# A cross-attention block: all of W1 by seven products, and PSUM as one tile

## The chip, the cores and the metric

The kernel runs on one core of a Trainium2 chip. The metric is the device time of one execution in microseconds (us). The engines named are TensorE (PE; its weight loads are shown apart as PEld), VectorE (DVE), ScalarE (ACT), GpSimd (POOL) and SyncE (SP, which only issues DMAs). All arithmetic is fp32.

## The reference

128 sequences of 128 tokens, 256 features, 16 heads of 16; a strictly causal mask (a token sees only earlier ones, and the first row of the attention is zero); two layer norms and a feed-forward part of width 1024.

```python
q = (query @ Wq + bq).reshape(b, s, 16, 16).transpose(0, 2, 1, 3)   # k, v from ctx alike
scores = jnp.einsum('bhqd,bhkd->bhqk', q, k) / sqrt(16)
scores = jnp.where(j < i, scores, -1e30)
attn = softmax(scores); attn[:, :, 0, :] = 0
ctx = jnp.einsum('bhqk,bhkd->bhqd', attn, v)
x = layer_norm(query + ctx @ Wo + bo, ln1_g, ln1_b)
ffn = jax.nn.relu(x @ W1 + b1) @ W2 + b2
out = layer_norm(x + ffn, ln2_g, ln2_b)
```

## The kernel before

The work goes by pairs of sequences, p = 0 to 63, 256 tokens each. Every engine's instructions run in the order of the program text (a manual schedule), with semaphores between engines; no engine runs anything ahead of what stands before it in its own queue. The stages of a pair are spread over several steps. `step(p)` is the steady part, for p = 7 to 62, and once more with `last` true for p = 63; in it stand

- `weigh(p-2)` and `context(p-2)`: attention weights times values into PSUM bank 7, copied by ScalarE;
- `scores_both(p)`: scores of pair p. The "high" half (queries 64 to 127 of each sequence) goes to banks 0 to 3, the "low" half (queries 0 to 63) to banks 6, 7, 4 and 5, four heads to a bank. TensorE writes banks 4 and 5 first, then 0 and 1, then 2 and 3, and 6 and 7 last;
- the masks and maxima on VectorE (`mask` for the low half, `mask_high` for the high half, `low_maximum`), and the exponentials by head on ScalarE, which also add up the sums of the softmax;
- projections: queries (bank 4) and keys (bank 0) of pair p+1, the attention's output of pair p-2 (bank 5), values of pair p (bank 1);
- `sums`: VectorE takes reciprocals, GpSimd multiplies the exponentials by them (the division of the softmax), in two parts of eight heads for the high half and in one for the low half;
- `turn`: VectorE transposes the weights in 32x32 blocks, twice for the high half (parts 0 and 1) and once for the low half; `bring` is 16 DMAs on SP's queue that finish this transposition, and it stands behind the `store` of an older pair;
- `norm1(p-2)` on ScalarE, and `turn_x1(p-2)`, a transposition of x1 on VectorE followed by five DMAs through DRAM;
- the feed-forward part. W2 of pair p-4 goes by seven products instead of eight (the Winograd form of Strassen's 2x2 scheme): GpSimd makes four sums `hS` of blocks of the hidden layer (`combine_hidden`), TensorE makes seven products of four 128x128x128 matmuls each into banks 6 and 7 (`second_by_seven`, with no-operations between the matmuls), VectorE adds them up (`sum_of_seven`). W1 of pair p-3 goes by seven products for half of its eight blocks of 128 hidden features: `NI = 2`, four sums `xS` of x1 on GpSimd (`combine_normed`), combinations `w1t` of the weights made once, products of two 128x128x128 matmuls, two products to a bank (banks 2 to 5; `Hidden.run`), and additions into `hT` on VectorE (`u2`, `u3`, `rest`). The other half of the blocks is plain, 256 columns at a time, into banks 0, 1, 2 and 0 (`Hidden.plain`). ScalarE applies bias and relu, to the plain blocks out of PSUM, to the others in place.

The relus of two of the blocks by seven products stand in the next step, behind `context`. PSUM's eight banks are eight tiles (`at_bank`). The steps ahead of 7 and the code behind 63 (`behind`) do the same work with other queues' orders.

Of the kernel before, what the change touches and what calls it, by code (L numbers as in the profile page):

```python
# [8 lines left out]
F32 = mybir.dt.float32  # L9
# [10 lines left out]
def tile_cross_attention_block(  # L20
# [188 lines left out]

    def at_bank(i, name):  # L210
        return psum.tile([P, 512], F32, tag=f"b{i}", name=name)
# [155 lines left out]
    def scores_both(p):  # L367

        st = states[p]
        for hi in range(2):  # L370
# [22 lines left out]
    def mask(p, hi, rs):  # L393
        st = states[p]
        n = P if hi else HP
        no = neg.rearrange("p u j -> p (u j)") if hi else neg[:, 1, :]
        for r in rs:
# [41 lines left out]


# [182 lines left out]
    b1s = const.tile([P, DFF // NS], F32, tag="b1s", name="b1s")  # L623
# [75 lines left out]
    def hidden(p, fs, between=None, banks=(2, 3, 4, 0)):  # L699
# [3 lines left out]
        for f in fs[::2]:  # L703
# [4 lines left out]
            for i in range(2):  # L708
                for k in range(KC):
# [5 lines left out]
                    if p == 1:  # L715
                        empty(3 if f else 2)
# [32 lines left out]
    def mask_high(p, rs):  # L749

        st = states[p]
        for r in rs:
            ps = st["sps", 1][r].rearrange("p (n j) -> p n j", j=P)
            nc.vector.tensor_tensor(
                ps[:, :, HP:], ps[:, :, HP:], neg[:, 1, None, :].to_broadcast([P, 4, HP]), ALU.add
            )
        for r in rs:
            nc.vector.tensor_reduce(  # L758
                st["nmx", 1][:, 4 * r : 4 * r + 4],
                st["sps", 1][r].rearrange("p (n j) -> p n j", j=P), AX.X, ALU.max, negate=True,  # L760
            )
# [5 lines left out]
    def exponential_by_head(p, hi, heads, summed=False):  # L767

        st = states[p]
        if summed and ("su", hi) not in st:  # L770
            st["su", hi] = small.tile([P, H], F32, tag=f"sa{hi}", name=f"sa{hi}_{p}")
# [28 lines left out]
    def second_by_seven(p):  # L800
# [3 lines left out]
        py = st["py"] = at_bank(6, f"py_{p}")  # L804
        pz = st["pz"] = at_bank(7, f"pz_{p}")
# [14 lines left out]
        product(py[:, :P], raw(0, 0), weights(0, 0), 7)  # L820
        product(pz[:, :P], raw(1, 0), weights(1, 0), 7)
        product(pz[:, 2 * P : 3 * P], raw(1, 1), lambda k: wt[:, 3, k], 7)
        product(py[:, 3 * P :], lambda k: hs[:, 0, k], lambda k: wt[:, 0, k], 7)
        product(py[:, 2 * P : 3 * P], lambda k: hs[:, 2, k], lambda k: wt[:, 2, k], 7)
        product(py[:, P : 2 * P], lambda k: hs[:, 1, k], lambda k: wt[:, 1, k], 7)
        product(pz[:, P : 2 * P], lambda k: hs[:, 3, k], weights(1, 1), 6)

    def sum_of_seven(p):

        st = states[p]  # L830
        t2 = st["t2"] = ffn.tile([P, 2, D], F32, tag="t2", name=f"t2_{p}", bufs=3)
        t = t2.rearrange("p s (h d) -> p (s h) d", h=2)
        py, pz = st.pop("py"), st.pop("pz")
        x1b = st.pop("x1b").rearrange("p s (h d) -> p (s h) d", h=2)
# [7 lines left out]
        add(t, x1b, 0)  # L842
# [7 lines left out]
    NI = 2  # L850
# [20 lines left out]
    class Hidden:  # L871

        WHERE = {1: (2, 0), 6: (2, 1), 7: (3, 0), 4: (3, 1), 2: (4, 0), 3: (4, 1), 5: (5, 0)}
# [8 lines left out]
        def of(self, which, n=1):  # L882
            at, n0 = self.WHERE[which]
            if at not in self.banks:
                self.banks[at] = at_bank(at, f"phs_{self.p}_{at}")
            return self.banks[at][:, n0 * NI * P : (n0 + n) * NI * P]

# [29 lines left out]
        def rest(self):  # L917
# [3 lines left out]
            )  # L921
            low = self.h[:, :, 0]
            nc.vector.tensor_tensor(
                low, low, self.of(2, 2).rearrange("p (e i t) -> p e i t", e=2, i=NI), ALU.add
# [49 lines left out]
    bvw = const.tile([P, KC, P], F32, tag="bvw", name="bvw")  # L974
# [257 lines left out]
    def fall_in(p):  # L1232

        weigh(p - 2)
        context(p - 2)
        scores_both(p)
        second_sum(1)
# [6 lines left out]
        mask_high(p, A)  # L1244
        exponential_by_head(p, 1, ONES)
        mask_high(p, B)
# [287 lines left out]
```

## Time and profile before

| | |
|---|---|
| time, median of 3 runs | 1520.04 us (1518.93 to 1522.97) |
| the profiled execution | 1522.34 us; its span, first to last instruction, 1520.5 us |
| mean granted clock of TensorE | 0.998 |
| busy share of the span | TensorE 99%, weight loads 89%, GpSimd 89%, ScalarE 85%, VectorE 84% |
| the largest parts of the chain that ended last | plain W1 (L938) 13%, W2 products (L809) 13% and 10%, W1 by seven products (L899) 11% |

In a row of a timeline stand the start in us, the duration, engine, line, operation, output and inputs, shapes and the count of instructions merged in it; in square brackets the idle time ahead of it and what ended that. A row of waits reads: who waited, for whom, us in total, times, the longest. One fp32 matmul stands as two records.

### The profile page before, as it was taken

What the parts mean: (1) busy time and instruction counts of PE and PEld (TensorE: products, weight loads), DVE (VectorE), ACT (ScalarE), POOL (GpSimd) and SP (SyncE); (2) the same over time, 40 slices, a digit from 0 to 9 for tenths busy, and PEclk for the clock granted to TensorE, in tenths of its full rate; (3) what the DMA queues carried; (4) which work ended last, traced back from release to release, by engine and by line L of the source; (5) the groups of instructions that cost most, each with busy time, mean ns of one, the idle gap of its engine ahead of it and who ended that gap; (6) DMA issues with size and microseconds to landing.
All of it is one profiled execution on the core that took longest, in us unless ns stands there. A gap on an engine that the chain in (4) does not pass through costs nothing.

```text
span 1520.5 us, 53525 instructions
## 1 busy us (share of the span) xinstructions
PE 1506.5 (99%) x18598; PEld 1359.2 (89%) x18598; DVE 1281.6 (84%) x2607; ACT 1295.0 (85%) x5271; POOL 1358.2 (89%) x1510
## 2 busy tenths in 40 slices
PE   8999999999999999999999999999999999999998
PEld 7788998999999989989989999899899899999987
DVE  7989888888888888888888888888888888888775
ACT  5668988988988989989889889899899898898862
POOL 6878999999999999999999999999999999999983
PEclk9999999999999999999999999999999999999999
DMA  9456665655655656656566566556565666664441
GB/s 196 91 113 144 147 151 139 138 133 135 141 142 138 131 140 135 147 138 135 134 137 142 141 140 129 142 133 150 134 140 131 139 137 146 138 132 124 108 119 47
DMA packets 415314, 204.59 MB, mean 135 GB/s; under 512 B 282448, under 2 KB 383056, under 8 KB 415056
## 3 DMA queue, kind: packets, MB, share of 16 engines
q1 hardware_dynamic: 412768, 199.34, 56.9%
q8 instruction: 158, 2.59, 0.8%
q10 hardware_dynamic: 2288, 1.85, 0.5%
q14 instruction: 100, 0.82, 0.2%
HBM read 70.26 MB, written 33.29 MB: 68 GB/s over the span
## 4 chain that ended last, share of the span: by engine, by line
PE 92%; DVE 3%; ACT 2%; POOL 1%; DMA 1%; SPq 1%; issue 1%; ACTq 0%; POOLq 0%; DVEq 0%
PE ph L938 13%; PE py L809 13%; PE phs L899 11%; PE pz L809 10%; PE pq L261 7%; PE po L523 7%; PE pv L301 7%; PE pk L261 6%; PE pss L384 6%; PE pc L504 4%; PE ph L710 3%; PE pc L494 2%; ACT sm L775 1%; SPq L462 1%; POOL sm L434 1%
## 5 line engine op out<-in xcount | busy, mean ns | idle before, releaser
L775 ACT ACTIVATE sm<-pss,nmx 128x128 f32<-128x128 f32 x944 | 328.5, 405 | 87.1 <-POOL hS L795 74.9
L434 POOL TENSOR_TENSOR sm<-sm,rs 128x1024 f32<-128x1024 f32 x192 | 362.1, 1900 | 3.4 <-DVE rs L433 3.3
L447 DVE STREAM_TRANSPOSE tb<-sm 128x1024 f32<-128x1024 f32 x186 | 223.4, 1226 | 110.9 <-POOL sm L434 90.7
L775 ACT ACTIVATE sm<-sm,nmx 128x64 f32<-128x64 f32 x944 | 313.7, 404 | 0.0
L775 ACT ACTIVATION_READ_ACCUMULATOR sm<-sm,nmx 128x1 f32 x912 | 235.1, 258 | 0.0
L775 ACT ACTIVATION_READ_ACCUMULATOR sm<-pss,nmx 128x1 f32 x912 | 223.3, 245 | 0.0
L938 PE MATMUL ph<-x1T,w 128*128 128x256 f32 x896 | 213.8, 386 | 0.1
L938 PEld LDWEIGHTS ph<-x1T,w 128*128 128x128 f32 x896 | 161.3, 190 | 36.1 <-ACT vd L324 18.8
L809 PE MATMUL py<-wt,hS 128*128 128x128 f32 x1440 | 171.2, 275 | 1.0 <-DVE hS L796 0.5
L809 PEld LDWEIGHTS py<-wt,hS 128*128 128x128 f32 x1440 | 165.8, 192 | 1.4 <-DVE hS L796 0.7
L758 DVE TENSOR_REDUCE nmx<-pss 128x4 f32<-128x512 f32 x236 | 150.9, 680 | 0.0
L398 DVE TENSOR_TENSOR sm<-pss,neg 128x256 f32<-128x256 f32 (+1 forms) x276 | 108.3, 435 | 34.9 <-PE pss L384 32.0
L928 ACT ACTIVATE hT<-ph,b1e_c 128x256 f32<-128x256 f32 x224 | 98.8, 465 | 35.5 <-PE ph L938 35.5
L291 ACT ACTIVATE kT<-pk,bkh,half 128x256 f32<-128x256 f32 x252 | 123.7, 609 | 4.0 <-PE pk L261 4.0
L261 PE MATMUL pq<-xT,wq 128*128 128x256 f32 x504 | 125.4, 392 | 0.5 <-DVE sm L398 0.5
L523 PE MATMUL po<-wo,cxT 128*128 128x256 f32 x512 | 121.3, 380 | 0.7 <-ACT cxT L516 0.7
L301 PE MATMUL pv<-wv,cT 128*128 128x256 f32 x512 | 120.9, 379 | 0.0
L261 PE MATMUL pk<-cT,wk 128*128 128x256 f32 x504 | 119.2, 379 | 0.0
L795 POOL TENSOR_TENSOR hS<-hT 128x512 f32<-128x512 f32 x57 | 72.2, 1267 | 50.2 <-ACT hT L928 50.1
L523 PEld LDWEIGHTS po<-wo,cxT 128*128 128x128 f32 x512 | 96.9, 190 | 14.4 <-ACT cxT L516 1.2
L261 PEld LDWEIGHTS pq<-xT,wq 128*128 128x128 f32 x504 | 90.7, 189 | 20.8 <-issue 9.8
L301 PEld LDWEIGHTS pv<-wv,cT 128*128 128x128 f32 x512 | 97.2, 190 | 13.2
(164 smaller groups left out, 3987.4 us busy)
## 6 DMA issues: line engine op xcount, KB each, us to landing
pT<-tb SPq DMA_DIRECT2D x976, 96.0 KB, 2.2
x1t<-tbx SPq DMA_DIRECT2D x252, 64.0 KB, 1.8
x1T<-x1t SPq DMA_DIRECT2D x63, 256.0 KB, 2.9
out_dram<-t SPq DMA_DIRECT2D x63, 256.0 KB, 2.4
xb<-in_x_dram SPq DMA_DIRECT2D x124, 128.0 KB, 3.8
cb<-in_ctx_dram SPq DMA_DIRECT2D x124, 128.0 KB, 3.8
x<-in_x_dram SPq DMA_DIRECT2D x31, 512.0 KB, 4.6
w<-in_L_xattn_W_dram SPq DMA_DIRECT2D x2, 1024.0 KB, 7.7
```

What stands on the lines that cost most here:

```text
L261: nc.tensor.matmul(ps[:, m * TP : (m + 1) * TP], w[:, k, m * P : (m + 1) * P], src[:, k, :], start=(k == 0), stop=(k == KC - 1),)
L291: nc.scalar.activation(st["kT"][:, m, e, :], pk[:, m * TP : (m + 1) * TP], AF.Identity, bias=bkh[:, m, e : e + 1], scale=half[:, e : e + 1],)
L301: nc.tensor.matmul(pv[:, s * D : (s + 1) * D], st["cT"][:, k, s * P : (s + 1) * P], wv[:, k, :], start=(k == 0), stop=(k == KC - 1),)
L398: nc.vector.tensor_tensor(st["sm", hi][:, 4 * r : 4 * r + 4, :], st["sps", hi][r][:, : 4 * n].rearrange("p (n j) -> p n j", j=n), no[:, No ...
L434: nc.gpsimd.tensor_tensor(sm[:, part, :], sm[:, part, :], rs[:, :, None].to_broadcast([P, part.stop - part.start, n]), ALU.mult,)
L447: nc.vector.transpose(st["tb"][:, :, at : at + 256].rearrange("p j (n a) -> p n j a", a=32), st["sm", hi].rearrange("p h j -> p (h j)")[:, ...
L523: nc.tensor.matmul(po[:, s * D : (s + 1) * D], cxT[:, k, s, :], wo[:, k, :], start=(k == 0), stop=(k == KC - 1),)
L758: nc.vector.tensor_reduce(st["nmx", 1][:, 4 * r : 4 * r + 4], st["sps", 1][r].rearrange("p (n j) -> p n j", j=P), AX.X, ALU.max, negate=True,)
L775: nc.scalar.activation(sm[:, h, :], src, AF.Exp, bias=nmx[:, h : h + 1], scale=1.0, **({"accum_out": st["su", hi][:, h : h + 1]} if summed ...
L809: nc.tensor.matmul(out, left(k), right(k), start=(k == 0), stop=(k == FC // 2 - 1))
L899: nc.tensor.matmul(ps[:, i * P : (i + 1) * P].rearrange("p (n a) -> p n a", a=32), left(i), right, start=True, stop=True,)
L938: nc.tensor.matmul(self.plains[f].rearrange("p (s i a) -> p s i a", s=2, a=32), w1[:, k, f * P : (f + 1) * P], self.x1T[:, :, :, k, :], st ...
```

## The change

- `NI = 4`: all eight blocks of W1 go by seven products, each product four 128x128x128 matmuls that fill one bank. The plain blocks are gone from the steps. `rest` is split in `add2`, `add3` and `add5`. The additions are twice as wide. Relus of the even blocks stand in the same step, those of the four odd blocks in the next one behind `context`.
- All of PSUM is one tile, `banks`, of which `at_bank` gives slices. With it the low mask of banks 6 and 7 is one instruction, and so are the mask and the maximum of the high half in banks 2 and 3; in banks 0 and 1 each maximum now follows its own mask.
- The first W2 product has bank 2 for itself and is added early (`first_of_seven`), ahead of the other sums.
- `sums` becomes `inverse` (one reciprocal for 16 heads) and `divide`. The order in the step changes: the high divisions stand ahead of the deviation and the shift of the first norm, `norm1` and `turn_x1` stand within the hidden stage, the low division behind `residual1`, `add_bo` behind the low division, the second high transposition ahead of the sums, the low one ahead of `add5`.
- Fewer no-operations in the W2 products (48 to 22 a step); two early tiles share the place of `hS`.

```diff
+    banks = psum.tile([P, 8, 512], F32, tag="banks", name="banks")
     def at_bank(i, name):
-        return psum.tile([P, 512], F32, tag=f"b{i}", name=name)
+        return banks[:, i]
...
+        if not hi and rs[0] == 0 and "both" in st:
+            r = rs[0]
+            at = (6, 4)[r // 2]
+            nc.vector.tensor_tensor(
+                st["sm", 0][:, 4 * r : 4 * r + 8, :].rearrange("p (b n) j -> p b n j", b=2),
+                banks[:, at : at + 2, : 4 * n].rearrange("p b (n j) -> p b n j", j=n),
+                no[:, None, None, :].to_broadcast([P, 2, 4, n]), ALU.add,
+            )
+            return
...
+    def inverse(p, hi):
+        st = states[p]
+        rs = st["rs", hi] = small.tile([P, H], F32, tag=f"rs{hi}", name=f"rs{hi}_{p}")
+        nc.vector.reciprocal(rs, st["su", hi])
+    def divide(p, hi, part):
+        st = states[p]
+        sm = st["sm", hi]
+        nc.gpsimd.tensor_tensor(
+            sm[:, part, :], sm[:, part, :],
+            st["rs", hi][:, part, None].to_broadcast([P, part.stop - part.start, sm.shape[2]]),
+            ALU.mult,
+        )
...
-    def mask_high(p, rs):
...
+    def mask_high(p, first, n):
+        st = states[p]
+        ps = banks[:, first : first + n].rearrange("p b (n j) -> p (b n) j", j=P)
+        nc.vector.tensor_tensor(
+            ps[:, :, HP:], ps[:, :, HP:], neg[:, 1, None, :].to_broadcast([P, 4 * n, HP]), ALU.add
+        )
+        nc.vector.tensor_reduce(
+            st["nmx", 1][:, 4 * first : 4 * (first + n)], ps, AX.X, ALU.max, negate=True,
+        )
...
-        product(py[:, :P], raw(0, 0), weights(0, 0), 7)
+        product(px[:, :P], raw(0, 0), weights(0, 0), 3)
...
+    def first_of_seven(p):
+        st = states[p]
+        st["t2"] = ffn.tile([P, 2, D], F32, tag="t2", name=f"t2_{p}", bufs=3)
+        nc.vector.tensor_tensor(
+            st["t2"].rearrange("p s (h d) -> p (s h) d", h=2),
+            st.pop("x1b").rearrange("p s (h d) -> p (s h) d", h=2),
+            st.pop("px")[:, None, :P].to_broadcast([P, 4, P]), ALU.add,
+        )
...
-    NI = 2
+    NI = 4
...
-        WHERE = {1: (2, 0), 6: (2, 1), 7: (3, 0), 4: (3, 1), 2: (4, 0), 3: (4, 1), 5: (5, 0)}
+        WHERE = {1: 2, 6: 3, 7: 4, 4: 5, 2: 0, 3: 1, 5: 6}
...
+        def add2(self):
+            nc.vector.tensor_tensor(self.h[:, 0, 0], self.h[:, 0, 0], self.one(2), ALU.add)
+        def add3(self):
+            nc.vector.tensor_tensor(self.h[:, 1, 0], self.h[:, 1, 0], self.one(3), ALU.add)
+        def add5(self):
...
         h.keep()
-        stack_values(p)
+        values_out(p)
         h.u2()
         h.run(7)
         h.run(4)
         h.u3()
+        norm1(p - 2)
+        norm2(p - 5)
+        turn_x1(p - 2)
         h.run(2)
+        h.add2()
         h.run(3)
+        h.add3()
+        for f in (0, 2, 4, 6):
+            h.relu(f)
+        turn(p, 0, 0)
         h.run(5)
-        h.rest()
-        norm2(p - 5)
-        h.plain([4], 0)
-        h.relu(4)
...
+        h.add5()
...
-            for f in range(NI, 2 * NI):
+            for f in (1, 3, 5, 7):
                 states[p - 4]["rest"].relu(f)
...
-        sums(p, 1, ONE)
-        sums(p, 1, TWO)
+        inverse(p, 1)
+        divide(p, 1, ONE)
+        divide(p, 1, TWO)
+        if not last:
+            deviation(p - 2, 1)
+            shift(p - 2, 1)
...
-        second_by_seven(p - 4)
+        second_by_seven(p - 4, None if last else 2)
         if not last:
-            sums(p, 0, ALL)
+            first_of_seven(p - 4)
+            turn(p, 1, 1)
         residual1(p - 3)
         sum_of_seven(p - 4)
-        if last:
-            sums(p, 0, ALL)
+        inverse(p, 0)
+        divide(p, 0, ALL)
         if not last:
-            turn_x1(p - 2)
-            spread_values(p)
+            add_bo(p - 1)
+        if not last:
             hidden_by_seven(p)
```

More of the change, by code (lines that the diff above doesn't have):

```diff
@@ L622, in tile_cross_attention_block @@
     b1e_c = const.tile([P, FC], F32, tag="b1e_c", name="b1e_c")
-    b1s = const.tile([P, DFF // NS], F32, tag="b1s", name="b1s")
+    early = ffn.tile([P, 4, FC // 2, P], F32, tag="hS", name="early", bufs=1)
+    b1s = early[:, 1, : DFF // NS // P].rearrange("p k f -> p (k f)")
     def fold_norm1():
@@ L804, in second_by_seven @@
         py = st["py"] = at_bank(6, f"py_{p}")
+        px = st["px"] = py if apart is None else at_bank(apart, f"px_{p}")
         pz = st["pz"] = at_bank(7, f"pz_{p}")
@@ L880, in __init__, with of @@
             self.banks, self.plains = {}, {}
[L882 to L886, printed above, removed]
+        def of(self, which):
+            if which not in self.banks:
+                self.banks[which] = at_bank(self.WHERE[which], f"phs_{self.p}_{which}")
+            return self.banks[which][:, : NI * P]
         def run(self, which):
@@ L972, in tile_cross_attention_block @@
     nc.vector.tensor_scalar(bqs_c, bq_c, QSCALE, None, ALU.mult)
-    bvw = const.tile([P, KC, P], F32, tag="bvw", name="bvw")
+    bvw = early[:, 0, :KC]
     nc.vector.memset(bvw[:, :, 0:1], 0.0)
@@ L1360, in step @@
         combine_hidden(p - 4, POOL_ALONE)
-        add_bo(p - 1)
-        if not last:
+        if last:
+            add_bo(p - 1)
+        else:
             combine_normed(p - 3)
@@ L1389, in step @@
         else:
-            norm1(p - 2)
             keys(p + 1)
             values(p)
-        sums(p, 1, ONE)
-        sums(p, 1, TWO)
+        inverse(p, 1)
+        divide(p, 1, ONE)
+        divide(p, 1, TWO)
+        if not last:
+            deviation(p - 2, 1)
+            shift(p - 2, 1)
         if p + 2 < NP:
@@ L1418, in step @@
             hidden(p - 3, range(FC))
-        turn(p, 0, 0)
-        if not last:
+        if last:
+            turn(p, 0, 0)
+        else:
             finish(p - 5)
@@ L1447, in behind @@
             scale_and_shift(p - 3)
+            finish(p - 4)
+            store(p - 4)
         norm2(p - 3)
```

75 lines of the change are left out of this document (27 added, 48 removed).

## The prediction

> **What bounds the kernel now.** First the page: how long, and which engine is busy.
>
> ```profile
> span 1520.5 us, 53525 instructions
> ...
> PE 1506.5 (99%) x18598; PEld 1359.2 (89%) x18598; DVE 1281.6 (84%) x2607; ACT 1295.0 (85%) x5271; POOL 1358.2 (89%) x1510
> ```
>
> TensorE is busy throughout, but its busy time is modelled, so I looked at one step of the steady part (`step(31)`) and at the whole steady part by windows.
>
> ```profile
> core 0: us, PE busy (x) PEld busy (x) DVE busy (x) ACT busy (x) POOL busy (x), PEclk, DMA share, GB/s
> 698.60:721.76 23.16, 23.16 (x293) 21.07 (x292) 19.78 (x42) 20.84 (x88) 21.44 (x25) 1.00 0.64 149
> 142.50:1439.71 1297.21, 1297.09 (x16353) 1179.95 (x16353) 1106.19 (x2294) 1166.34 (x4927) 1198.17 (x1345) 1.00 0.60 137
> ```
>
> From 142.50 to 1439.71 the kernel makes the 56 steps of p = 7 to 62 in 1297.21 us, 23.16 each, at full clock, and the step shown takes exactly that. The waits inside that step, by who sat idle, for VectorE and GpSimd:
>
> ```profile
> DVE tb L447 <- POOL sm L434: 1.9, 1, 1.9
> DVE sm L398 <- PE pss L384: 0.5, 1, 0.5
> DVE hT L911 <- ACT hT L908: 0.3, 1, 0.3
> POOL hS L795 <- ACT hT L928: 0.9, 1, 0.9
> ```
>
> TensorE has no row there; the others wait for it or for each other: VectorE 2.7 us of 23.16, GpSimd 0.9. So TensorE's own stream sets the step, but GpSimd's queue is full to 22.26 and VectorE's to 20.46. TensorE's timeline of the step, and one weight-load row:
>
> ```profile
> 698.29 0.38 PE L938 MATMUL ph<-x1T,w 128*128 128x256 f32 x1
> 698.60 0.43 PE L494 MATMUL pc<-pT,vd 128*32 128x64 f32 x16
> ...
> 701.63 1.99 PE L261 MATMUL pq<-xT,wq 128*128 128x256 f32 x8
> 703.46 1.89 PE L523 MATMUL po<-wo,cxT 128*128 128x256 f32 x8
> 705.19 1.89 PE L261 MATMUL pk<-cT,wk 128*128 128x256 f32 x8
> ...
> 714.00 1.06 PE L809 MATMUL pz<-w,hS 128*128 128x128 f32 x8
> 714.89 0.61 PE L899 MATMUL phs<-x1T,w 128*128 128x128 f32 x4
> ...
> 718.02 3.82 PE L938 MATMUL ph<-x1T,w 128*128 128x256 f32 x16
> 721.76 0.43 PE L494 MATMUL pc<-pT,vd 128*32 128x64 f32 x16
> 718.98 2.46 PEld L938 LDWEIGHTS ph<-x1T,w 128*128 128x128 f32 x12 [0.33 <-ACT vd L324]
> ```
>
> Read the starts. One fp32 matmul is two records. 128 columns: 8 records from 714.00 to 714.89, 0.112 us each. 256 columns: 8 from 703.46 to 705.19, 0.216 each. W1 is the stretch 714.89 to 721.76.
>
> **TensorE's part of the change.** Removed are the 16 wide records of the plain blocks (718.02 to 721.76, 3.74 us); added are 28 narrow ones, as many as stand in 714.89 to 718.02, so 3.13 us. Of the 3.74, 3.46 is 16 x 0.216. Some of the rest is the wait for the values' copies (0.33 on the weight loads, `vd`, bank 1), which goes; the rest is the hand-over to the next stage, 698.29 to 698.60 = 0.31 against 0.216, so 0.09, which stays. Gain 3.74 - 3.13 - 0.09 = **0.52 us a step, floor 22.64**. The product that now takes bank 1 after the values comes 4.5 us into W1, where the second plain block came after 4.1, and norm1 no longer stands ahead of those copies. The no-operations in the W2 products, cut from 48 to 22 a step, I cost at nothing either way: 8 padded records (714.00) and the unpadded W1 records stand equally 0.112 apart.
>
> **VectorE.** Rows of the same step:
>
> ```profile
> 700.89 0.76 DVE L398 TENSOR_TENSOR sm<-pss,neg 128x256 f32<-128x256 f32 x2 [0.53 <-PE pss L384]
> 706.05 1.22 DVE L765 TENSOR_REDUCE nmx<-sm 128x16 f32<-128x1024 f32 x1
> 709.15 0.66 DVE L247 STREAM_TRANSPOSE xT<-xb 128x512 f32<-128x512 f32 x1
> 718.85 0.42 DVE L914 TENSOR_TENSOR hT<-hT,phs 128x256 f32<-128x256 f32 x1
> 719.83 0.69 DVE L919 TENSOR_TENSOR hT<-hT,phs 128x512 f32<-128x512 f32 x1
> 720.56 0.69 DVE L923 TENSOR_TENSOR hT<-hT,phs 128x512 f32<-128x512 f32 x1
> 721.16 2.36 DVE L447 STREAM_TRANSPOSE tb<-sm 128x1024 f32<-128x1024 f32 x2
> ```
>
> Three additions into `hT` go from 256 to 512 elements (0.42 to 0.69): +0.81. L919 goes from 512 to 1024; no 1024 addition from PSUM is in the trace: between 1.22 (the 1024 reduction) and 2 x 0.69 = 1.38. I take 1.22, since 256 to 512 added only 0.27: +0.53. L923 becomes two of its size: +0.69. Together +2.03. Saved: one mask, one mask and one maximum of the high half, one reciprocal, at most 0.1 each, since two masks back to back take 0.76 against 0.69 for one double one; given back, because each high maximum now follows its own mask at once. I count zero. VectorE needs 20.46 + 2.03 = 22.5 of 22.64: it fits by 0.15, so its order decides.
>
> The **VectorE loop**: the query projection writes bank 4, so it waits for the low mask, which stands behind all that VectorE has from the step before. From 701.63 to the first W1 record at 714.89 is 13.26; four products of 8 records 3.58; the last record outlives its successor's start by 0.17 (1.06 against 0.89); hand-over 0.08. At 17.09 VectorE may do the second half of u3, and behind it in its queue: transposition of x1 0.60 (0.66 of L247, less what two rows overlap where nothing is waited for: 720.56 + 0.69 against 721.16), add2 0.60 (720.56 to 721.16), add3 0.66, the last low transposition 1.18 (half of 2.36), add5 1.21, masks 0.76; u3's half itself 0.70 (its row has 0.69). Sum 5.71, **22.80 a step**. All these instructions are on the path; beside them run TensorE's last three W1 products, the weighing and the scores (2.7 + 0.1 + 3.0).
>
> The first W2 product goes to bank 2, which the first W1 product needs at 714.89, so its early addition must be over by then. VectorE queues it behind the first high transposition, which waits for a division. That division ends about 711.6 (first `hS` 0.9 later than now, 702.6, + 5.0 + 1.9 + 1.9, rows below); transposition 1.2, addition 0.63: 713.5. It has 1.4 to spare and costs nothing; later than that, TensorE waits for all of it.
>
> **GpSimd.** The same operations in another order:
>
> ```profile
> 701.68 1.27 POOL L795 TENSOR_TENSOR hS<-hT 128x512 f32<-128x512 f32 x1 [0.87 <-ACT hT L928]
> 706.71 1.27 POOL L254 TENSOR_TENSOR xb<-x,bov_r 128x512 f32<-128x512 f32 x1
> 707.94 0.46 POOL L866 TENSOR_TENSOR xS<-x1T 128x128 f32<-128x128 f32 x1
> 709.86 0.23 POOL L543 TENSOR_SCALAR ve<-mv 128x2 f32<-128x2 f32 x1
> 711.43 3.75 POOL L434 TENSOR_TENSOR sm<-sm,rs 128x1024 f32<-128x1024 f32 x2
> 715.27 0.22 POOL L543 TENSOR_SCALAR ve<-mv 128x2 f32<-128x2 f32 x1
> 716.85 1.90 POOL L434 TENSOR_TENSOR sm<-sm,rs 128x1024 f32<-128x1024 f32 x1
> 718.71 1.27 POOL L577 TENSOR_TENSOR x1b<-x,g_r 128x512 f32<-128x512 f32 x1
> 721.28 1.30 POOL L608 TENSOR_TENSOR t<-t,g_r 128x512 f32<-128x512 f32 x1
> 700.70 0.91 ACT L928 ACTIVATE hT<-hT,b1e_c 128x256 f32<-128x256 f32 x2
> ```
>
> The **GpSimd loop** is new: add5 touches every odd block, so four relus instead of two wait for it, and the first `hS` for them. Relus: two take 0.91, two more 0.82: 1.73. `hS` 701.68 to 706.71 = 5.03, `xS` 707.94 to 709.86 = 1.92, high divisions 711.43 to 715.27 = 3.84, two deviations with shifts 1.57 + 1.58, residual 718.71 to 721.28 = 2.57 (now ahead of the low division), low division 1.90: 18.41. Then the low transposition 1.18, behind it add5 1.22, four hand-overs 0.2. Sum **22.74**. The sum of xb (1.23) and the finishing (2.65) run beside that. The high divisions come 2.8 earlier in GpSimd's own order (xb and a deviation no longer precede them), 1.9 net of the later `hS`, so most of VectorE's 1.9 of idling goes; that pays for the +2.03.
>
> **ScalarE.** It makes the same count of relus and copies, one copy 256 wider; it ran 20.84 busy and has two microseconds of room. norm1 now follows the values' copies, so x1's transposition and its DMAs move late. SP's queue and the landing:
>
> ```profile
> 701.33 12.03 SPq L462 DMA_DIRECT2D pT<-tb  x16
> 721.69 0.38 SPq L242 DMA_DIRECT2D x1T<-x1t  x1
> x1T<-x1t SPq DMA_DIRECT2D x63, 256.0 KB, 2.9
> ```
>
> x1T landed at 721.69 + 2.9 = 724.6; `xS` reads it at 707.94 + 23.16 - 1.2 = 729.9. Four microseconds later would still be hidden; I expect 2.5. The store waits for the finishing and starts about 1.4 later, with the 16 DMAs (to 713.4) behind it; their data is wanted at 721.76, so that costs nothing either.
>
> **Sum.** The longest loop is 22.80: 23.16 - 22.80 = 0.36, x 56 = 20.2 us. Outside: twice as wide W1 sums once at the start (4 x 0.54 on GpSimd, bounds 0 and 2.2) and two more relus ahead of the exponentials in the last step (0 to 0.8): I take 1. So -19. The profiled execution took 1522.34 (span 1520.5), 2.3 over the median of the runs, 1520.04; the difference is taken from the median: **1501 us**. About 0.3% (4.6 us) is what this measurement can tell from no change.
>
> **Rivals.**
> (a) TensorE stays alone in front: VectorE's semaphores cost less than I count and the loops close under 22.64, which takes 0.16 off the VectorE loop. For it: L923 starts 0.04 after L919 ends, though it too has waits. 56 x 0.52 = 29, so 1491 to 1492. 0.26.
> (b) The VectorE loop eats it all: add5 at 1.38 and 0.04 more at each of five semaphores gives 23.16, 1520. 0.10.
> (c) Slower: the GpSimd loop. I counted 0.05 for a hand-over; the trace's 0.3 for `hT` from ScalarE (L911) is the other bound. At 0.3 for each of four it is 23.74, x 56 = +32; at 0.2, 23.34, +10. It decides from 23.16, that is 0.15 a hand-over. Middle 1541. 0.12. Against: GpSimd started at 701.68, about 0.07 behind the relus (700.70 + 0.91).
> (d) Narrow matmuls limited by their weight loads:
>
> ```profile
> L899 PEld LDWEIGHTS phs<-xS,w1t x672: 192/192/192, 159.1 to 1435.7; 128*128 128x128 f32 x168
> ```
>
> If a narrow record cost its 0.192 load, 28 added ones would take 5.4 instead of 3.13, W1 would lose 1.7 a step, +97 us, 1617. Speaking against: 28 of just this form stand 0.112 apart. 0.02. [...]
> (e) The single PSUM tile is ordered as a whole and not by bank; then every engine waits for every other, and the step nears the sum of TensorE's and VectorE's work, 43 us, 2600 in all. The slices are by bank; 0.02.
>
> **How the numbers follow.** Forecast 0.48, (a) 0.26, (b) 0.10, (c) 0.12, (d) and (e) 0.04. Range 1490 to 1520: forecast, (a) and most of (b), 0.81. Faster by over 0.3%: 0.48 + 0.26 + 0.02 of (b) = 0.76; within: 0.08; slower 0.16.
>
> **What would show it.** Right: 56 W1 records 0.112 apart in 6.26 us; no wait for `vd` on weight loads; steps of 22.7 to 22.9; TensorE now waiting 0.1 to 0.2 a step ahead of L261 or the low scores, for VectorE; VectorE's idle before its first high transposition under 0.7; add5 1.2. Wrong: steps at 22.64 (a); GpSimd without any wait before `hS` and VectorE idling before the last low transposition (c); narrow records over 0.15 apart (d).

## The result, and the profile after

The changed kernel takes 1494.36 us (median of 4 runs, 1492.56 to 1495.45), the kernel before 1519.59 beside it (1518.93 to 1522.97): a ratio of 0.9828, 95% interval 0.9811 to 0.9846, so 25.2 us faster where 19 were forecast. The profiled execution of the changed kernel took 1494.63 us. The page's span line and busy times:

```profile
span 1492.9 us, 53293 instructions
...
PE 1478.8 (99%) x19270; PEld 1376.9 (92%) x19270; DVE 1379.4 (92%) x2428; ACT 1321.3 (89%) x5271; POOL 1359.7 (91%) x1510
```

VectorE rises from 84 to 92%, with fewer instructions (2428 for 2607): the work moved as the prediction says, from TensorE's wide products to VectorE's additions. The answer by windows, one step of the steady part (counted from 144.64 it is `step(47)`) and the 56 steps p = 7 to 62, in the columns of the same view in the prediction:

```profile
1050.87:1073.51 22.64, 22.64 (x306) 21.40 (x305) 21.55 (x39) 21.37 (x89) 21.43 (x25) 1.00 0.65 152
144.64:1413.07 1268.43, 1268.15 (x17025) 1198.39 (x17024) 1206.05 (x2126) 1192.76 (x4929) 1197.03 (x1343) 1.00 0.60 140
```

A step is 22.64 us, not 22.80. The 56 steps fell from 1297.21 to 1268.43, by 28.8; the profiled executions differ by 1522.34 - 1494.63 = 27.7, so the rest of the kernel lost 1.1. Between the medians it is 25.2 because the profiled execution of before lay 2.8 over its median and that of after only 0.3 over its own.

The waits inside that step, VectorE's two and GpSimd's one; TensorE again has no row:

```profile
DVE tb L474 <- DMA pT<-tb: 0.2, 1, 0.2
DVE hT L949 <- PE banks L933: 0.2, 1, 0.2
POOL hS L820 <- ACT hT L964: 0.4, 1, 0.4
```

VectorE waited 2.7 us a step before, 1.9 of it for a division ahead of the first high transposition; 0.4 is left. TensorE's timeline of the step:

```profile
1050.87 0.43 PE L521 MATMUL banks<-pT,vd 128*32 128x64 f32 x16
1051.12 0.63 PE L531 MATMUL banks<-pT,vz 128*32 128x64 f32 x32
1051.57 0.41 PE L521 MATMUL banks<-pT,vd 128*32 128x64 f32 x16
1051.79 0.63 PE L531 MATMUL banks<-pT,vz 128*32 128x64 f32 x32
1052.35 1.62 PE L387 MATMUL banks<-kT,qT 32*64 32x128 f32 x64
1053.90 1.99 PE L263 MATMUL banks<-xT,wq 128*128 128x256 f32 x8
...
1066.27 1.06 PE L835 MATMUL banks<-w,hS 128*128 128x128 f32 x8
1067.16 1.06 PE L933 MATMUL banks<-x1T,w 128*128 128x128 f32 x8
1068.05 1.95 PE L933 MATMUL banks<-xS,w1t 128*128 128x128 f32 x16
...
1073.51 0.43 PE L521 MATMUL banks<-pT,vd 128*32 128x64 f32 x16
```

W1 is now 1067.16 to 1073.51, 6.35 us: 56 records at 0.112 (6.26) and the hand-over of 0.09. It took 6.87 before. The 0.52 saved is the whole difference of the step, 23.16 to 22.64. Half of the step's matmul records, 160 of 304 (the view's 306 has two of the step before), stand in the first 3.03 us, the weighing (L521, L531) and the scores (L387); that matters for the first experiment. VectorE and GpSimd in the same step:

```profile
1051.93 1.18 DVE L959 TENSOR_TENSOR hT<-hT,banks 128x1024 f32<-128x1024 f32 x1
1053.15 0.76 DVE L411 TENSOR_TENSOR sm<-banks,neg 128x256 f32<-128x256 f32 x2
...
1061.48 0.22 DVE L457 RECIPROCAL rs<-sa 128x16 f32<-128x16 f32 x1
...
1064.13 1.25 DVE L474 STREAM_TRANSPOSE tb<-sm 128x1024 f32<-128x1024 f32 x1 [0.22 <-DMA pT<-tb]
1065.30 0.65 DVE L858 TENSOR_TENSOR t<-x1b,banks 128x512 f32<-128x512 f32 x1
...
1070.93 0.69 DVE L949 TENSOR_TENSOR hT<-hT,banks 128x512 f32<-128x512 f32 x1 [0.20 <-PE banks L933]
1071.54 0.70 DVE L702 STREAM_TRANSPOSE tbx<-x 128x512 f32<-128x512 f32 x1
1072.17 0.65 DVE L952 TENSOR_TENSOR hT<-hT,banks 128x512 f32<-128x512 f32 x1
1072.74 0.67 DVE L955 TENSOR_TENSOR hT<-hT,banks 128x512 f32<-128x512 f32 x1
1073.40 1.25 DVE L474 STREAM_TRANSPOSE tb<-sm 128x1024 f32<-128x1024 f32 x1
1074.57 1.18 DVE L959 TENSOR_TENSOR hT<-hT,banks 128x1024 f32<-128x1024 f32 x1
1075.79 0.42 DVE L411 TENSOR_TENSOR sm<-banks,neg 128x256 f32<-128x256 f32 x1
```

```profile
1054.93 1.27 POOL L820 TENSOR_TENSOR hS<-hT 128x512 f32<-128x512 f32 x1 [0.36 <-ACT hT L964]
...
1061.32 0.46 POOL L904 TENSOR_TENSOR xS<-x1T,xS 128x128 f32<-128x128 f32 x1
1061.78 3.75 POOL L462 TENSOR_TENSOR sm<-sm,rs 128x1024 f32<-128x1024 f32 x2
...
1071.46 1.91 POOL L462 TENSOR_TENSOR sm<-sm,rs 128x1024 f32<-128x1024 f32 x1
```

Three loops can be read from these rows: chains of work through several queues that come back, one step later, to where they began. The odd addition is `add5` (L959), which waits for the last product and touches all four odd blocks; the early addition is `first_of_seven` (L858).

**The GpSimd loop** (forecast 22.74): first `hS` to the end of the low division, 1054.93 to 1073.37, is 18.44 (forecast 18.41); the low transposition begins 0.03 later, the odd addition 1.17 after that, it takes 1.18, and from its end, 1075.75, to the next `hS`, one step after 1054.93, are 1.82, the four relus among them. Sum 22.64.

**The VectorE loop** (forecast 22.80): the query projection starts at 1053.90, the second half of u3 at 1070.93, 17.03 later; from there to the next mask 4.86, and the first mask itself 0.42: 22.31. So the mask that TensorE waits for is done 0.33 before TensorE comes to it.

**A third loop**, which the prediction does not have: from the end of the odd addition, 1053.11, VectorE's masks, maxima and norm statistics to the end of the high reciprocal, 1061.70, 8.59; the high divisions begin at 1061.78, 0.08 later (and directly behind the last `xS`); to the end of the low division 11.59; then 0.03, 1.17 and 1.18 to the end of the next odd addition. Sum 22.64.

So by these rows TensorE's stream, the GpSimd loop and the third loop all take as long as the step. A loop that merely keeps pace with TensorE shows a wait somewhere; GpSimd's 0.36 for the relus is one, the 0.08 ahead of the high divisions may be another, and whether they are slack or a loop closing the rows do not tell. The experiments do.

### The profile page after: what moved, and what is told of

Same layout as the page of the kernel before. It is cut to its first block, busy times and chain, and to the rows that moved or that the text cites. A ratio compares the mean times of both kernels' runs of the same rounds, so it can differ in the third digit from the quotient of the medians.

```text
span 1492.9 us, 53293 instructions
## 1 busy us (share of the span) xinstructions
PE 1478.8 (99%) x19270; PEld 1376.9 (92%) x19270; DVE 1379.4 (92%) x2428; ACT 1321.3 (89%) x5271; POOL 1359.7 (91%) x1510
## 4 chain that ended last, share of the span: by engine, by line
PE 89%; DVE 4%; ACT 3%; POOL 2%; issue 1%; DMA 1%; ACTq 0%; SPq 0%; POOLq 0%; DVEq 0%
PE banks L835 24%; PE banks L933 23%; PE banks L263 14%; PE banks L550 7%; PE banks L303 7%; PE banks L387 6%; PE banks L531 3%; PE banks L521 2%; PE banks L738 2%; ACT sm L800 1%; DVE su L445 1%; PE banks L758 0%; ACT hT L746 0%; DVE sm L411 0%; DVE tb L474 0%
## 5 line engine op out<-in xcount | busy, mean ns | idle before, releaser
L800 ACT ACTIVATE sm<-banks,nmx 128x128 f32<-128x128 f32 x944 | 329.0, 377 | 20.9 <-DVE nmx L784 11.2
L964 ACT ACTIVATE hT<-hT,b1e_c 128x256 f32<-128x256 f32 x448 | 191.3, 497 | 28.8 <-DVE hT L952 22.8
L800 ACT ACTIVATION_READ_ACCUMULATOR sm<-banks,nmx 128x1 f32 x912 | 197.8, 217 | 0.0
L835 PE MATMUL banks<-wt,hS 128*128 128x128 f32 x1440 | 170.7, 275 | 0.1
L933 PE MATMUL banks<-xS,w1t 128*128 128x128 f32 x1344 | 168.4, 275 | 0.0
L835 PEld LDWEIGHTS banks<-wt,hS 128*128 128x128 f32 x1440 | 165.6, 192 | 0.3 <-DVE hS L820 0.3
L784 DVE TENSOR_REDUCE nmx<-banks 128x4 f32<-128x512 f32 x177 | 153.8, 869 | 6.0
L933 PEld LDWEIGHTS banks<-xS,w1t 128*128 128x128 f32 x1344 | 159.1, 192 | 0.0
L293 ACT ACTIVATE kT<-banks,bkh,half 128x256 f32<-128x256 f32 x252 | 122.0, 584 | 4.0 <-PE banks L263 4.0
L263 PE MATMUL banks<-xT,wq 128*128 128x256 f32 x504 | 125.4, 392 | 0.0
L263 PE MATMUL banks<-cT,wk 128*128 128x256 f32 x504 | 119.2, 379 | 0.0
```

Of the source, the lines that this page charges most:

```text
L263: nc.tensor.matmul(ps[:, m * TP : (m + 1) * TP], w[:, k, m * P : (m + 1) * P], src[:, k, :], start=(k == 0), stop=(k == KC - 1),)
L293: nc.scalar.activation(st["kT"][:, m, e, :], pk[:, m * TP : (m + 1) * TP], AF.Identity, bias=bkh[:, m, e : e + 1], scale=half[:, e : e + 1],)
L784: nc.vector.tensor_reduce(st["nmx", 1][:, 4 * first : 4 * (first + n)], ps, AX.X, ALU.max, negate=True,)
L800: nc.scalar.activation(sm[:, h, :], src, AF.Exp, bias=nmx[:, h : h + 1], scale=1.0, **({"accum_out": st["su", hi][:, h : h + 1]} if summed ...
L835: nc.tensor.matmul(out, left(k), right(k), start=(k == 0), stop=(k == FC // 2 - 1))
L933: nc.tensor.matmul(ps[:, i * P : (i + 1) * P].rearrange("p (n a) -> p n a", a=32), left(i), right, start=True, stop=True,)
```

## The experiments

Theory, after the two traces: three ceilings lie together at 22.63, so taking work from TensorE gains nothing and adding to VectorE or GpSimd costs all or nearly all of it. Rival: TensorE alone is in front, and the others have room. Each kernel was timed beside the kernel before on the same chip. Where a step's time is given without a row it is the distance between two starts of L521 (L494 in the kernels made from before).

### The no-operations of before

```
-        product(px[:, :P], raw(0, 0), weights(0, 0), 3)
+        product(px[:, :P], raw(0, 0), weights(0, 0), 7)
...   # the other five 3 -> 7, the last 4 -> 6
```

> The changed kernel with the no-operations of the W2 products put back from 22 to 48 a step; nothing else. Prediction's own step (no-operations cost nothing either way): the steady step stays 22.63 us, the time 1492 to 1497. Rival: each of the 26 takes TensorE's queue about 0.02, then the step is 23.1 and the time about 1523, and part of the gain was theirs.

Measured: 1506.82 us (ratio 0.9908, 0.9893 to 0.9922). The expectation was wrong. Of 55 steps 39 take 22.63 to 22.64; 16 take 22.70 to 24.04. By windows, a long step between its two neighbours, then TensorE's weight loads' waits in the long one:

```profile
717.36:740.00 22.64, 22.64 (x306) 21.40 (x305) 21.63 (x39) 21.31 (x89) 21.43 (x25) 1.00 0.57 131
740.00:763.71 23.71, 23.02 (x305) 21.41 (x305) 21.77 (x39) 21.43 (x89) 22.49 (x26) 1.00 0.62 147
763.71:786.35 22.64, 22.64 (x306) 21.40 (x305) 21.54 (x39) 21.32 (x89) 20.39 (x25) 1.00 0.57 130
```

```profile
PEld banks L387 <- issue: 1.1, 1, 1.1
```

The clock is full in all three, and the 1.1 us stand in the scores (L387), released by nothing the profile knows. In the W2 products, where the no-operations are, nothing changed: from the first of them to W1 it is 6.25 us, as in after. What differs from after is the count: TensorE has 640 records a step in the traces of before and after, no-operations included, and 666 here. The page of after lists a queue "instruction" with its transfers, MB and share of the time, and that of the kernel with 48 no-operations the second row:

```profile
q8 instruction: 158, 2.59, 0.8%
...
q8 instruction: 164, 2.69, 0.8%
```

In the trace of after each of the 158 has 16,384 bytes. The traces have 40,530 and 42,090 records of TensorE, so 256.5 and 256.6 to a transfer; the 1560 more records of this kernel come with 6 more transfers, and in after the starts of two transfers lie 256.1 TensorE records apart on average. One transfer is counted here as a block of 256. 640 is two and a half such blocks, so in after the steps begin by turns at records 108 and 236 of a block, all along (before: 110 and 238), counted from the first TensorE record of the trace. With 666 the place drifts. Sorted by it, the steps that begin at 134 to 154 are the long ones (23.36 to 24.04), those at 186 to 194 take up to 23.04, and nearly all others 22.63.

That the borders cost the long steps their time is so far the author's guess. Two kernels below test the place by itself.

### Two of four matmuls of the fifth W1 product left out

```
-            for i in range(NI):
+            for i in range(NI if which != 5 else 2):
```

> The changed kernel with two of the four matmuls of W1's fifth product left out (that part of the sum then uses what the bank held), 0.45 us of TensorE a step. Theory T1 (the VectorE and the GpSimd loop are as long as TensorE's stream within 0.05): the step stays at 22.58 to 22.64, the time 1491 to 1495. Theory T2 (TensorE alone sets the step, the others have room and only follow closely): the step falls to 22.19, the time to about 1469.

Measured: 1495.62 us (0.9834, 0.9819 to 0.9849). With less work for TensorE the kernel is no faster. But its steps have 632 records, so they drift too: most take 22.42 to 22.63 and 12 of 55 up to 23.55. The second part of that hides what the first is worth, so it was repeated with the count kept:

```
             for i in range(NI if which != 5 else 2):
                 nc.tensor.matmul(
                 ...
+            if which == 5:
+                empty(8)
```

> Two of the four matmuls of the fifth W1 product are left out again, now with 8 no-operations in their place, so that a step keeps 640 TensorE instructions and the block borders stay. TensorE has 0.45 us less a step. If the loop of GpSimd and VectorE is as long as TensorE's stream (22.60 to 22.62): steps of 22.60, 1491 to 1495 with no longer ones among them. If TensorE alone held the step: 22.2 to 22.4, 1470 to 1483.

Measured: 1493.28 us (0.9818, 0.9799 to 0.9837), 52 of 55 steps at 22.62 to 22.65 and none over 22.70. The wait of TensorE's weight loads, over the whole run (total, times, longest):

```profile
PEld banks L387 <- DVE hT L961: 16.4, 56, 0.3
```

Where TensorE has less to do its weight loads wait 0.3 us in each of the 56 steps, in the scores, for the odd addition (L961 here, L959 in after): W1 is 0.45 shorter (5.90 for 6.35), from the start of the scores to the query projection it takes 0.45 longer (2.00 for 1.55), and the step stays 22.64. That is the GpSimd or the third loop, which both end in that addition. "TensorE alone" would have given 22.2 to 22.4: refuted.

### One low mask done twice

```
-        mask(p, 0, B)
+        mask(p, 0, B if last else (2, 2, 3))
```

> The changed kernel with one of the two low masks ahead of the query projection made twice in each steady step (the same values again): 0.34 us more on VectorE, in the loop that the prediction summed at 22.80. T1: the whole 0.34 shows, step 22.93 to 22.99, time 1511 to 1515. T2: step under 22.70, time under 1499.

Measured: 1514.04 us (0.9953, 0.9938 to 0.9968), steps of 22.98 on average. VectorE's masks and what follows them, then the waits of the weight loads and of GpSimd over the run:

```profile
952.55 1.20 DVE L411 TENSOR_TENSOR sm<-banks,neg 128x256 f32<-128x256 f32 x3
953.66 0.42 DVE L781 TENSOR_TENSOR banks<-banks,neg 128x256 f32<-128x256 f32 x1
```

```profile
PEld banks L263 <- DVE sm L411: 20.9, 57, 0.4
POOL sm L462 <- DVE rs L457: 17.5, 55, 0.3
```

The three masks stand 1.11 before the next instruction where two stood 0.68 (1053.15 to 1053.83); of the 0.43 added, 0.34 show in the step. TensorE waits for the mask, and GpSimd's division waits 0.3 for the reciprocal, which it did not before. The VectorE loop of 22.31 would have had room for 0.33 and come to 22.74; the third loop gives 22.64 + 0.43 = 23.07 at most. 22.98 needs the third, and puts it at 22.98 - 0.43 = 22.55: it is 0.09 short of the step in after, not quite as long.

### One GpSimd sum done twice

```
-        nc.gpsimd.tensor_tensor(xs[:, 0], x1T[:, 1, :, 0, :], x1T[:, 1, :, 1, :], ALU.add)
+        for _ in range(2):
+            nc.gpsimd.tensor_tensor(xs[:, 0], x1T[:, 1, :, 0, :], x1T[:, 1, :, 1, :], ALU.add)
```

> The changed kernel with the first xS sum made twice on GpSimd in each steady step (the same values again), 0.41 us, between hS and the high divisions. If GpSimd's loop (add5, four relus, hS, xS, divisions, low transposition, add5) is as long as the step, the whole 0.41 shows: step 23.0 to 23.06, time 1514 to 1519. If only its queue counted (0.36 idle ahead of hS): 22.68, time about 1497. If TensorE alone sets the step: 22.63.

Measured: 1523.43 us (0.9997, 0.9987 to 1.0006): half a microsecond of GpSimd undoes the whole change. The steps average 23.14. GpSimd's timeline and the weight loads' waits:

```profile
964.41 0.99 POOL L902 TENSOR_TENSOR xS<-x1T 128x128 f32<-128x128 f32 x2
965.36 0.46 POOL L903 TENSOR_TENSOR xS<-x1T 128x128 f32<-128x128 f32 x1
```

```profile
PEld banks L387 <- DVE hT L960: 19.3, 55, 0.4
```

The pair takes 0.95 start to start where the single one takes 0.42 (1059.96 to 1060.38 in after); the added 0.53 was expected at 0.4, and 0.50 shows. The loop through GpSimd is 23.14 - 0.53 = 22.61 long in after, so it has next to no slack, although GpSimd still waits 0.37 a step for the relus: that wait is the loop closing.

### The seven products for all blocks, alone

The kernel before with `NI = 4`, a bank for each product, and nothing else of the change (two initial tiles share memory to make room):

```
-    NI = 2
+    NI = 4
...
-        WHERE = {1: (2, 0), 6: (2, 1), 7: (3, 0), 4: (3, 1), 2: (4, 0), 3: (4, 1), 5: (5, 0)}
+        WHERE = {1: 2, 6: 3, 7: 4, 4: 5, 2: 0, 3: 1, 5: 6}
...
-        h.plain([4], 0)
-        h.relu(4)
...
```

> The kernel before with W1 by seven products for all blocks and nothing else of the change (banks 2, 3, 4, 5, 0, 1, 6 for the products; the order of the queues, eight PSUM tiles, the single masks, the reciprocals, the late first sum and the 48 no-operations as before). T1: the orders pay for it; the high divisions come late on GpSimd, VectorE waits for them and has 2.0 more behind them, then eight relus: 11.7 + 9.9 + 3.9, step 24.8 to 25.6, time 1610 to 1655. T2: TensorE sets the step, 22.64 to 22.8, time 1491 to 1502.

Measured: 1622.83 us (1.0672, 1.0654 to 1.0689), steps of 24.94. VectorE's and GpSimd's waits in one step:

```profile
DVE tb L447 <- POOL sm L434: 2.4, 1, 2.4
POOL hS L796 <- ACT hT L928: 2.7, 1, 2.7
```

The arithmetic that saves TensorE 0.52 costs 1.78 a step while the queues keep their order: GpSimd waits 2.7 for the relus, VectorE then 2.4 for the division. Each of its steps takes 24.94 to 24.96, so the drift of its 668 records a step shows in none of them. Of what this kernel lacks, the joined masks and the early addition are worth 0 and 0.1 a step (below); what makes the change a gain is the order of the queues.

### GpSimd's old order

The kernel after with xb's sum ahead of the masks and the first norm's deviation and shift ahead of the high divisions, as before:

```
-        if last:
-            add_bo(p - 1)
-        else:
+        add_bo(p - 1)
+        if not last:
...
+        deviation(p - 2, 1)
+        shift(p - 2, 1)
         if last:
...
```

> The changed kernel with GpSimd's order of before in one respect: the sum of xb and the deviation and shift of the first norm stand ahead of the high divisions again. Theory T1: the divisions end 2.8 later, VectorE's first high transposition waits for them with everything to add5 behind it; 0.45 of that is covered today; step 24.7 to 25.1, time 1610 to 1635. Rival: VectorE has other work to fill it or GpSimd is not in the path: step under 23.2, time under 1527.

Measured: 1622.16 us (1.0645, 1.0629 to 1.0661), steps of 24.95 on average. TensorE's timeline:

```profile
1034.59 1.16 PE L933 MATMUL banks<-x1T,w 128*128 128x128 f32 x8 [1.29 <-DVE t L858]
```

These two moves alone are worth 2.3 us a step. The high divisions come late, so the first high transposition does, and the early addition behind it; the first W1 product waits 1.29 for its bank. Of the 2.31, 1.45 stand between the first W2 product and W1, 0.76 in the scores, whose weight loads now wait 0.6 for the odd addition, and 0.10 in W1. It is the case that the prediction named at the early addition: later than the start of W1, TensorE waits for all of it.

### The first W2 product added with the others

```
-        second_by_seven(p - 4, None if last else 2)
+        second_by_seven(p - 4)
         if not last:
-            first_of_seven(p - 4)
```

> The changed kernel with the first W2 product back in bank 6 and added with the other sums, behind the second high transposition; the rest as changed. VectorE's work is the same, but 0.6 of it moves behind a wait for the seven products. T1: second transposition 0.25 later at most, step 22.63 to 22.8, time 1492 to 1504. Rival: the early addition is what makes the change pay, step 23.1 or more, time over 1520.

Measured: 1500.00 us (0.9842, 0.9827 to 0.9857), steps of 22.73 on average. The early addition is worth 0.1 a step, 5 to 6 us; the 0.1 stands in the scores (1.65 from their start to the query projection's, 1.55 in after). These steps have 639 records and drift too, but all 55 take 22.71 to 22.75.

### The low transposition behind the odd addition

```
-        turn(p, 0, 0)
         h.run(5)
         h.add5()
+        turn(p, 0, 0)
```

> The changed kernel with the low transposition behind add5 instead of ahead of it. add5 then waits for W1's last product, about 0.3 of VectorE's idling that the transposition now fills, in the loop to the query projection; GpSimd's loop gets 1.2 shorter. T1: step 22.8 to 22.95, time 1503 to 1512. If GpSimd's loop is the one that holds the step: 22.63 or less. If TensorE alone does: 22.63.

Measured: 1494.08 us (0.9807, 0.979 to 0.9823), steps of 22.63: not 22.8. The transposition had been thought to delay TensorE from its new place. Its rows:

```profile
959.43 0.67 DVE L955 TENSOR_TENSOR hT<-hT,banks 128x512 f32<-128x512 f32 x1
960.22 1.22 DVE L959 TENSOR_TENSOR hT<-hT,banks 128x1024 f32<-128x1024 f32 x1
961.35 1.24 DVE L474 STREAM_TRANSPOSE tb<-sm 128x1024 f32<-128x1024 f32 x1
```

Both still end ahead of the masks, in either order, and the odd addition waits only 0.12 for its product (960.22 against the end of its predecessor, 959.43 + 0.67). The order inside this pair is free. The expectation's rule, that whoever stands last pays, was wrong here. The run shows one thing more. The odd addition no longer stands behind the low division, so the GpSimd loop does not close there, the third is shorter by the 1.2 of the odd addition, and the step is the same, with TensorE busy for all of it: TensorE's stream alone takes 22.63. With the fifth product cut short (above) GpSimd's loop alone gave 22.64. The two ceilings are within a few hundredths of each other.

### The masks and maxima bank by bank

```
-        if not hi and rs[0] == 0 and "both" in st:
+        if False:
...
+        for r in range(first, first + n):
+            ps = banks[:, r].rearrange("p (n j) -> p n j", j=P)
+            ...   # all masks of the call, then all its maxima, a bank each
```

> The kernel after with each mask and each maximum on one bank again, the high ones in the order mask, mask, maximum, maximum, the low ones one by one. If TensorE's own stream holds the step, and the loop through masks, inverse, divisions, low transposition and the odd addition was no longer before (there the masks reached the inverse 0.2 us sooner): steps of 22.63, 1492 to 1497. If the joined masks are what lets the loop close: VectorE loses 0.1 to 0.3 us a step: 22.7 to 22.9, 1498 to 1510.

Measured: 1494.11 us (0.9815, 0.98 to 0.9829), steps of 22.63. The joined masks, which the single PSUM tile makes possible, move nothing. That agrees with the zero the prediction counted for them.

### The place of the instruction blocks

Two kernels with 640 records a step as in after, but other places of the borders, by no-operations far ahead of the steps:

```
-                        empty(3 if f else 6)
+                        empty(3 if f else 10)   # the other kernel: empty(3 if f else 2)
```

> The kernel after with 32 more no-operations once, in the W1 products of the second pair (6 each becomes 10), 100 us before the steady part; the steps keep their 640 TensorE instructions. If the place of the borders of TensorE's instruction blocks (256 instructions, 16,384 bytes) decides, steps that began at instruction 108 and 236 of a block now begin at 140 and 12: those at 140 take 23.3 to 24.0 us as the steps at 134 to 154 did with 48 no-operations, the others 22.63; 28 such steps, 20 to 35 us in all: 1515 to 1530. If the number of no-operations in a step was what cost, nothing changes: 1493 to 1497.

> The kernel after with the 32 no-operations taken back that it adds once in the second pair's W1 products (6 becomes 2, as before the change). Steps then begin at instruction 76 and 204 of a block. If the place of the block borders decides: both places were clean in the kernels whose places drift, so steps of 22.63 and 1492 to 1497, and the 32 added instructions were not needed. If blocks must begin where they did before the change (110 and 238): over 1500.

In before the line has `empty(3 if f else 2)`: the change itself adds these no-operations, and the second kernel takes them back. The line stands in a loop that passes four times with f = 0, so the shift was 16 and not 32 as expected: steps begin at 124 and 252, and at 92 and 220. (The page agrees: 53309 instructions in the first for 53293 in after.) The place 140 was not reached.

Measured: 1499.64 us (0.9856, 0.984 to 0.9871) for 16 on and 1496.90 (0.9832, 0.9818 to 0.9847) for 16 back; their runs lie at 1499.04 to 1503.16 and 1495.51 to 1498.03, those of the kernel with single masks, which begins its steps at 109 and 237, at 1493.86 to 1494.34 on the same chip. With 16 on, the 27 steps from 252 average 22.64, the 28 from 124 22.79, up to 23.49. With 16 back, those from 92 average 22.63 and those from 220 22.75, up to 23.02. In after both kinds average 22.64. Groups by line (times, busy us in total, mean ns, idle before), the query projection (L263) and the scores (L387) in after; then the scores with 16 back, the query projection with 16 on, and the scores with 48 no-operations a step:

```profile
L263 PE MATMUL banks<-xT,wq 128*128 128x256 f32 x504 | 125.4, 392 | 0.0
...
L387 PE MATMUL banks<-kT,qT 32*64 32x128 f32 (+1 forms) x3840 | 98.7, 330 | 0.8 <-ACT hT L746 0.8
```

```profile
L387 PE MATMUL banks<-kT,qT 32*64 32x128 f32 (+1 forms) x3840 | 101.6, 331 | 0.9 <-ACT hT L746 0.8
```

```profile
L263 PE MATMUL banks<-xT,wq 128*128 128x256 f32 x504 | 128.5, 395 | 1.4 <-issue 0.9
```

```profile
L387 PE MATMUL banks<-kT,qT 32*64 32x256 f32 (+1 forms) x3840 | 105.7, 331 | 6.9 <-issue 5.7 <-ACT hT L746 0.8
```

With the same instructions and work in a step and only 16 no-operations less or more once, the scores take 2.9 us more, or the projection behind them 3.1 and 1.4 of idling. With 48 in each step the scores lose 7.0 and 6.1 of idling, 13.1 together, which is the 12.5 and a little more. So the place of the borders costs time by itself, and the number of no-operations in a step does not need to. The size, 20 to 35 us, was expected for a place that was not reached; that 134 to 154 would cost it at 640 records is not shown. "Over 1500 with the 16 taken back" is refuted too. Where TensorE stands is on record. In all 11 steps from 134 to 154 with 48 no-operations, and in all 13 of 22.75 and over with 16 on, its longest pause is ahead of the same record of a block, 193 in the counting above; the five steps of 23.0 with 16 back lose 0.30 to 0.32 there. The pauses recur every 256 records, as borders do. Why some borders cost and others nothing is argued only: half the step's TensorE instructions run in its first 3.03 us, so a block can be used up there in some 2.4 us (an estimate, 256 of 320 instructions), and a transfer of one took 0.9 to 1.7 in the trace of after. In the steps from 134 to 154 the block that ends at the pause does run off inside that stretch; but so it does in a step from 188, which took 22.64. The cause stays open.

## Why the prediction was right, and where it was off

**The floor** came out as worked out: gain 3.74 - 3.13 - 0.09 = 0.52, floor 22.64, measured 22.64; the 28 added narrow records stand 0.112 apart and the hand-over stayed 0.09. `vd`'s wait is gone. Rival (d) is out with that.

**The likeliest case was not the one that came true.** The step is at TensorE's floor, as in rival (a), which gave 1491 to 1492; the forecast of 22.80 was 0.16 too long, 9 us over 56 steps, and 1.1 outside was about the 1 taken. The failed step is the VectorE loop, two of its terms. "Masks 0.76": the query projection needs only the first of the two, done after 0.42. "u3's half itself 0.70": its row is 0.69 long, but the next instruction starts 0.61 after it. These two take 0.34 and 0.09 off; the second half of u3 starting at 17.03 instead of 17.09 takes 0.06, and the sum is 22.31 instead of 22.80. Rival (a)'s reason, cheaper semaphores, is 0.05 of that (u3 starts 0.03 behind its product, 0.08 was counted); it was not what closed the loop.

**The GpSimd loop** was right in mechanism and 0.1 too long: 18.44 for 18.41 in its own queue, 4.20 for 4.33 behind. It is a bound, as the doubled sum shows, but at 22.61 and not, as rival (c) allowed, at 23.3 or more. The price of a hand-over was near the low end: 0.03 from the division to the transposition.

**Left out:** the third loop, in which VectorE's masks to the reciprocal and GpSimd's divisions to the odd addition are chained. The prediction treats VectorE and GpSimd as two separate loops; the doubled mask shows that the chain through both is 22.55 long, longer than the 22.31 of the VectorE loop that the forecast was made from. That it cost nothing is luck: nothing in the prediction kept it under TensorE's 22.64.

**"+2.03 for VectorE, paid by the 1.9 of idling"** held in the main: 19.78 busy became 21.55, which is +1.77, and the idling before the first high transposition fell from 1.9 to 0.22. Taking the order away (GpSimd's old one) or never making it (the products alone) gives 24.95 and 24.94.

**The early addition** "has 1.4 to spare and costs nothing": it ends at 1065.95, W1 starts at 1067.16, 1.2 to spare. (The prediction's terms for the division ahead of it add up to 711.4, where it wrote 711.6.) The prediction did not say that it gains; without it a step is 0.1 longer.

**The odd addition** of 1024 elements, taken at 1.22 between 1.22 and 1.38, took 1.18. **The single PSUM tile** is not ordered as a whole: rival (e) is out.

**The no-operations** "at nothing either way" was right for their own time and wrong for the kernel's: put back to 48 a step they cost 12.5 us, half of the gain, with the borders of the instruction blocks at another place in each step. The 26 that the change drops from a step stand against 12 more matmuls and 12 more weight loads (672 and 671 more in the 56 steps) and two more records of semaphores, so that the trace has 640 TensorE records a step before and after. The prediction had no term for this; that the change keeps the count is, as far as the forecast goes, luck.

None of the kernels that leave nothing out was measurably faster than the change: the single masks (1494.11) and the moved transposition (1494.08) are the same within their intervals, and TensorE's stream, the GpSimd loop and the third loop would have to be shortened together.

## What to carry to other kernels

When a change takes work from the engine in front, work out each closed loop through the other queues with start-to-start distances, follow the chain that crosses from one engine to another and back, and ask of a paired instruction which half the waiter needs. A doubled cheap instruction is the quickest test whether a wait that the profile shows is slack or a loop closing: GpSimd waited 0.4 a step and yet had none. In an unrolled kernel at an engine's floor, count that engine's instructions per step before adding or removing any: here 26 no-operations more in each step, with the same work, cost 12.5 us.

## What was not expected of the hardware

In the traces of this case TensorE's records go with transfers of 16,384 bytes, one to 256 of them: 158 for 40,530 in after, 164 for 42,090 with 48 no-operations. At their borders in or just behind a dense stretch (here 160 of the step's 304 matmul records in 3.03 us) TensorE stood for up to 1.4 us with no releaser in the trace ("issue"): with 48 no-operations 16 waits of the weight loads in the scores, 11.3 us together. At most borders it did not: in after 55 of the 56 steps, each with two or three borders, took 22.63 to 22.68. With the work of a step unchanged, 16 no-operations less or more ahead of the steady part cost 2.8 and 5.5 us in 1494, and 26 more in each step 12.5. So two of these kernels that differ by a few TensorE instructions are compared fairly only if this is looked at.
